# A routed expert kernel on one core: six single tiles computed in three steps of two tiles, with the routing's steps placed anew

## The chip, the core and the metric

One NeuronCore of a Trainium2 chip. Its engines run side by side and wait for each other by semaphores: TensorE (PE; matmuls, with their weight loads shown as PEld), VectorE (DVE), ScalarE (ACT), GpSimd (POOL) and SyncE (SP). The metric is the device time of one execution in microseconds (us). The kernel before takes 427.55 us, the median of 3 runs (427.18 to 428.36).

## The reference

The input x has 64 sequences of 64 tokens with 256 features, so 4096 tokens. A gate of eight experts is read from a normalised x and from a second input, each token takes the two experts of the highest gate, and their three-layer networks' outputs, weighted by the gate, are added to x:

```python
xn = rms_w * (x * jax.lax.rsqrt(var + EPS))
gate = xn @ wg_W + wg_b + (genre_embed @ gg_W + gg_b)
gate_w = jax.nn.softmax(gate, axis=-1)
topk_w, topk_i = jax.lax.top_k(gate_w, TOP_K)
cw = jnp.sum(jax.nn.one_hot(topk_i, E, dtype=x.dtype) * topk_w[..., None], axis=-2)
h1 = jax.nn.relu(jnp.einsum('bsh,ehm->bsem', x, W1) + b1)
h2 = jax.nn.relu(jnp.einsum('bsem,emn->bsen', h1, W2) + b2)
out_e = jnp.einsum('bsen,enh->bseh', h2, W3) + b3
return jnp.einsum('bseh,bse->bsh', out_e, cw)
```

W1 is 256 x 512 for each expert, W2 512 x 512 and W3 512 x 256, all in float32.

## The kernel before

Only the two chosen experts of a token are computed. Tokens of one expert are gathered into tiles of 128 rows. The kernel has a head and a tail.

The **head** first routes part A, 8 of the 32 groups of 128 tokens, which already gives two full tiles for each of the experts 1, 4 and 7. These are the six **single tiles** 0 to 5 (F = 6, HALF = 2 for each expert). Each goes through `layer1`, `layer2` and `layer3` in plain float32, where one matmul of the program leaves two records in the trace. `layer1` and `layer2` make the transposed hidden rows, four blocks m or n of 128 features, each in its own PSUM bank (PB0 to PB3), which a relu on ScalarE moves to `hid[0]` or `hid[1]`. `layer3` reads `hid[1]` as the stationary operand, and `give` on VectorE scales the result, which GpSimd later adds to the output by an indirect DMA. The rows of a tile come by a gather on GpSimd, two transposes on PE (`transpose_x`, L951) and a copy on ScalarE (L952).

Between the single tiles the routing of **part B**, the other 24 groups, is done. It is a generator, `rest()`, which a call of `more()` (the name `routing` at the top) moves on by a step. Its chain: choice of the experts on VectorE; the `ranks` and `totals`, small matmuls on PE (L433, L434, L439); VectorE's sums from L716 on, which give each entry a slot, in two halves `lo` and `hi`; four chunks c = 0 to 3 of one-hot operands on VectorE (L756, L757, L760), for which ScalarE widens `hi` (`wides`, L772) and token numbers (`tokw`, L679); 64 table matmuls on PE (L675), which sum these into one PSUM bank; then `idxR`, the token of each slot, by which unit F's rows are gathered. A transposed and turned copy `idxG` (PE L786, VectorE L802) serves the gathers of F+1 and later units, and eight steps on VectorE (L787 to L804) find the number `nex` of the first of 40 prepared shapes that fits the counts of tiles. It selects the arm of a switch in which the tail stands.

The **tail** computes the remaining tiles in **units** F, F+1, ... of up to four tiles, 512 columns. Its matmuls are float32r with split operands: high, low and a combination (`near`, L1139, and `cross`, L1154, for layers 1 and 2, `near3` and `cross3` for the third). For unit F, `transpose_part` transposes gathered rows on PE (L1190), ScalarE makes the high part (L1191) and VectorE the low part (L1192) and the combination; `split_w1` and `split_w2` split the weights (ScalarE L1081, VectorE L1084 and L1087). Units after F are transposed by two DMAs through device memory (`stow`, L926, and `shuffle`, L934) and one VectorE instruction (L943). `scales` takes the gathered gate weights, GpSimd gathers and adds throughout.

No scheduler decides the order: `tc.manual_schedule()` takes the instructions of each engine as they are written. Engines run them in that order, so a waiting instruction holds up what stands behind it on its engine. The head is written in `head_step(u, more)` for tiles 0 to 4 and `bridge()` for tile 5; each does `layer1(u)`, then `layer3(u - 1)`, then `layer2(u)`, with steps of the routing between. `layer3(5)` stands in unit F's `row`.

## Time and profile before

| | before |
|---|---|
| median of 3 runs | 427.55 us (427.18 to 428.36) |
| the profiled execution | 428.56 us |
| its span in the trace | 426.7 us |
| PE busy | 410.3 us (96%) |
| DVE, ACT, POOL busy | 343.2 (80%), 258.2 (61%), 314.0 us (74%) |
| mean granted clock of PE | 0.988 |
| share of PE in the chain that ended last | 92% |

The profile is one execution. The span runs from the first to the last instruction, and 1.86 us of the execution's time lie outside it. The start of an instruction is recorded; the end of a matmul is modelled. The granted clock is a share of 2.4 GHz. A row of the chain or of a timeline merges neighbours of one kind: "x8" are eight records. A bracket holds the idle time of the engine before the instruction and what ended it.

### The profile page before, as it was taken

How to read it: one execution, taken by the hardware profiler on the slowest of the kernel's cores; microseconds unless marked ns; L12 is line 12 of the kernel's file. 1: busy time of each engine (PE TensorE's matmuls, PEld its weight loads, DVE VectorE, ACT ScalarE, POOL GpSimd, SP SyncE). 2: the span in 40 equal slices, each digit the busy share in tenths (PEclk: the TensorE clock that was granted, in tenths of full speed). 3: DMA queues.
4: the chain of work that ended last, by engine and by line, in shares of the span. 5: the costliest groups of instructions: out<-in, count | busy, mean ns of one | idle time of the engine just before them, and what ended most of it. 6: DMA issues, size and time to landing. Idle time of an engine off the chain costs nothing.

```text
span 426.7 us, 7483 instructions
## 1 busy us (share of the span) xinstructions
PE 410.3 (96%) x2525; PEld 374.5 (88%) x2525; DVE 343.2 (80%) x545; ACT 258.2 (61%) x502; POOL 314.0 (74%) x243
## 2 busy tenths in 40 slices
...
GB/s 305 253 305 385 354 196 63 135 97 144 193 149 132 112 239 113 130 190 137 187 55 201 126 191 56 262 41 200 83 222 61 179 147 177 175 35 13 44 37 41
DMA packets 68241, 65.77 MB, mean 154 GB/s; under 512 B 35922, under 2 KB 57300, under 8 KB 67812
## 3 DMA queue, kind: packets, MB, share of 16 engines
...
## 4 chain that ended last, share of the span: by engine, by line
PE 92%; issue 2%; DMA 2%; POOL 1%; DVE 1%; ACT 1%; POOLq 0%; ACTq 0%
PE pb L1139 38%; PE pb L1154 19%; PE pb L1232 13%; PE pb L1252 6%; PE pb L1068 5%; PE pb L1056 3%; PE pb L1219 3%; POOL out_dram L1294 1%; PE pb L278 1%; DMA big<-in_x_dram 1%; PE pb L675 1%; DMA xg<-in_x_dram,idxA 1%; PE pb L309 1%; ACT pb L1147 1%; PE pb L951 0%
## 5 line engine op out<-in xcount | busy, mean ns | idle before, releaser
L1147 ACT ACTIVATE pb<-pb,bb 128x384 f32<-128x384 f32 (+7 forms) x136 | 79.5, 599 | 93.1 <-PE pb L1139 88.5
L883 POOL DMA_INDIRECT cg<-cwdR,idxR x61 | 93.1, 1527 | 18.6 <-issue 16.8
L1139 PE MATMUL pb<-h1h,w2h 128*128 128x384 f32 (+7 forms) x272 | 97.7, 360 | 0.0
L1139 PE MATMUL pb<-h1l,w2l 128*128 128x384 f32 (+7 forms) x272 | 97.4, 359 | 0.0
L1294 POOL DMA_INDIRECT out_dram<-ysE,idxR x31 | 58.3, 1881 | 11.8 <-issue 4.9
L1294 POOL DMA_INDIRECT out_dram<-ysO,idxR x27 | 49.1, 1818 | 16.1 <-ACT ysO L1275 8.1
L1179 DVE SCALAR_TENSOR_TENSOR h2l<-pb,h2h 128x384 fp32r<-128x384 f32 (+7 forms) x64 | 39.2, 617 | 26.8 <-ACT h2h L1166 19.5
L1154 PE MATMUL pb<-h1d,w2d 128*128 128x384 f32 (+7 forms) x272 | 56.4, 359 | 0.0
L1232 PE MATMUL pb<-w3h,h2h 128*128 128x256 f32 (+6 forms) x232 | 56.0, 282 | 0.0
L1232 PE MATMUL pb<-w3l,h2l 128*128 128x256 f32 (+6 forms) x232 | 56.0, 282 | 0.0
L1139 PEld LDWEIGHTS pb<-h1h,w2h 128*128 128x128 f32 x272 | 51.1, 188 | 4.4
L1139 PEld LDWEIGHTS pb<-h1l,w2l 128*128 128x128 f32 x272 | 51.2, 188 | 4.3
L1154 PEld LDWEIGHTS pb<-h1d,w2d 128*128 128x128 f32 x272 | 49.0, 188 | 4.8
L1139 PE MATMUL pb<-xh,w1h 128*128 128x384 f32 (+7 forms) x136 | 49.1, 362 | 0.4 <-ACT hid L1071 0.4
L1139 PE MATMUL pb<-xl,w1l 128*128 128x384 f32 (+7 forms) x136 | 48.7, 359 | 0.0
L883 POOL DMA_INDIRECT xgE<-in_x_dram,idxG x31 | 37.9, 1222 | 9.8 <-issue 8.8
L1166 ACT ACTIVATE h2h<-pb 128x384 fp32r<-128x384 f32 (+7 forms) x64 | 34.5, 540 | 16.8 <-PE pb L1154 13.3
L1232 PEld LDWEIGHTS pb<-w3l,h2l 128*128 128x128 f32 (+6 forms) x232 | 42.9, 185 | 0.4
L1232 PEld LDWEIGHTS pb<-w3h,h2h 128*128 128x128 f32 (+6 forms) x232 | 42.9, 185 | 0.3
L1179 DVE SCALAR_TENSOR_TENSOR h1l<-pb,h1h 128x384 fp32r<-128x384 f32 (+7 forms) x68 | 36.7, 601 | 2.4 <-ACT h1h L1163 2.3
L883 POOL DMA_INDIRECT xgO<-in_x_dram,idxG x27 | 30.2, 1119 | 8.2 <-issue 7.9
L1154 PE MATMUL pb<-xd,w1d 128*128 128x384 f32 (+7 forms) x136 | 31.9, 369 | 2.3 <-ACT pb L1147 2.2
...
## 6 DMA issues: line engine op xcount, KB each, us to landing
...
```

Source lines behind the costliest of these rows:

```text
L883: return nc.gpsimd.indirect_dma_start(out=dst, out_offset=None, in_=src, in_offset=bass.IndirectOffsetOnAxis(ap=index(b) if at is None els ...
L1056: nc.tensor.matmul(ph, lhsT=w1[:, c, ts(m, P)], rhs=cols[:, c, :], start=(c == 0), stop=(c == HC - 1))
L1068: nc.tensor.matmul(ph, lhsT=w2[:, m, ts(n, P)], rhs=hid[0][:, m], start=(m == 0), stop=(m == MC - 1))
L1139: nc.tensor.matmul(bank, lhsT=ws[t][:, c, ts(n, P)], rhs=xs[t][:, c, 0 : width(u)], start=c == 0 and t == 0, stop=c == k - 1 and t == 1, s ...
L1147: nc.scalar.activation(bank, bank, AF.Identity, bias=ww[u][1][:, l, n : n + 1], scale=1.0 + 1.0 / FINE)
L1154: nc.tensor.matmul(bank, lhsT=ws[2][:, c, ts(n, P)], rhs=xs[2][:, c, 0 : width(u)], start=False, stop=c == k - 1, skip_group_check=True,)
L1166: nc.scalar.activation(room["h2"][0][:, n, 0 : width(u)], bank, AF.Relu, scale=NEAR)
L1179: V.scalar_tensor_tensor(l, PB[n][:, 0 : width(u)], 0.0, plain(h), ALU.max, ALU.subtract)
L1219: nc.tensor.matmul(sums(u, k)[0 : cols.stop - cols.start], lhsT=native(u)[:, n, cols], rhs=w3[:, n, :], start=(i == 0), stop=(i == MC - 1),)
L1232: nc.tensor.matmul(sums(u, k)[0 : cols.stop - cols.start], lhsT=room["h2"][t][:, n, cols], rhs=room["w3"][t][:, n, :], start=n == 0 and t ...
L1252: nc.tensor.matmul(sums(u, k)[0 : cols.stop - cols.start], lhsT=room["h2"][2][:, n, cols], rhs=room["w3"][2][:, n, :], start=False, stop=n ...
L1294: add = nc.gpsimd.indirect_dma_start(out=orows, out_offset=bass.IndirectOffsetOnAxis(ap=index(b)[0 : y.shape[0]], axis=0), in_=y, in_offse ...
```

## The change

- `hid` holds 256 columns. `head_step`, `third_part` and `bridge` go, and one function `singles(more)` has the head's order. `layer1` and `layer2` take a pair q of tiles, 2q and 2q+1, 256 columns at a time; the first pair's layer 1 is done in two halves of 128 columns, since tile 1's rows come later. `layer3` of both tiles of a pair follow each other, except that `layer3(5)` still stands in unit F's row.
- The ranks and totals stand inside the second pair's layer 1 (before: inside tile 1's layer 2). The table's matmuls stand ahead of the third pair's layer 1 (16), after it (16), and after `layer3(3)` (32).
- The weights of part B's tokens are taken ahead of the last one-hot chunk. The shapes lie on 40 partitions, so the branch's steps are four on VectorE, before the table's last part; a small matmul L793 of the new file brings the marks to one row, and the turned index, the priority and `nex` follow after `idxR`.
- Unit F's second half of transposes uses PB0 and PB1; the splits of its W1 and W2 stand earlier. Adds are ordered by pairs, and gathers of x and gate weights are asked for in another order. Two more warm-up matmuls of 128 columns stand at the program's start.

```diff
-    hid = [wall.tile([P, MC, BT], F32, name=f"hid{k}") for k in range(2)]
+    hid = [wall.tile([P, MC, HALF * BT], F32, name=f"hid{k}") for k in range(2)]
...
-    shp = head.tile([1, NS, 2 * E + 1], F32, name="shp")
+    shp = head.tile([NS, 2 * E + 1], F32, name="shp")
...
-        for n in (TPB, TPB, TPB, TPB, TPB, TPB, 2, 1):
+        for n in (TPB, TPB, TPB, TPB, TPB, TPB, 2, 1, 1, 1):
...
-        prio, vm, okk = (buf(gx, [1, n], a) for a, n in (("prio", 1), ("vm", NS), ("okk", NS)))
-        viol = buf(gx, [1, NS, E], "viol")
+        prio, vm, okk = (buf(gx, [P, 1], a) for a in ("prio", "vm", "okk"))
+        viol = buf(gx, [P, 2 * E], "viol")
...
+            if c == NCH - 1:
+                pB.weights()
+                pB.spread(cwdR, cw8B, 0)
...
-        pB.weights()
-        nc.gpsimd.tensor_copy(cw8B[:, 0:NA, :], pA.cw8)
-        pB.spread(cwdR, cw8B, 0)
-        yield
-        table()
-        V.tensor_scalar(sa, tab, 0.0, float(NT + 1), ALU.is_le, ALU.mult)
-        V.scalar_tensor_tensor(idxR, tab, -1.0, sa, ALU.add, ALU.add)
-        gather_unit(F)
-        yield
-        turned, idxf = PB[7][:, P : P + NREST], t2("idxf", NREST)
-        V.tensor_copy(idxf, idxR)
-        nc.tensor.matmul(turned, lhsT=swap, rhs=idxf, start=True, stop=True)
         V.tensor_scalar(hf_i, mm, float(WQ - 1), None, ALU.add)
         V.tensor_reduce(rank, cmp, AX.X, ALU.add)
         V.tensor_scalar(hf_i, hf_i, WQ.bit_length() - 1, None, ALU.arith_shift_right)
@@ -791,17 +775,25 @@
         V.tensor_copy(hf, hf_i)
         V.tensor_tensor(cmp, hot, across(hf), ALU.mult)
         V.tensor_reduce(sL, cmp, AX.X, ALU.add)
-        near = sL[0:1].unsqueeze(1).to_broadcast([1, NS, E])
-        upper, lower = (shp[:, :, k * E : k * E + E] for k in (0, 1))
-        V.tensor_tensor(viol, near, upper, ALU.is_gt)
-        V.tensor_reduce(vm, viol, AX.X, ALU.max)
-        V.scalar_tensor_tensor(okk, vm, 0.0, shp[:, :, 2 * E], ALU.is_equal, ALU.mult)
-        V.tensor_tensor(viol, near, lower, ALU.is_le)
-        V.tensor_reduce(vm, viol, AX.X, ALU.max)
-        V.scalar_tensor_tensor(okk, vm, 0.0, okk, ALU.is_equal, ALU.mult)
+        some_viol, some_vm, some_okk, some_sL = viol[0:NS], vm[0:NS], okk[0:NS], sL[0:NS]
+        V.tensor_tensor(some_viol[:, 0:E], some_sL, shp[:, 0:E], ALU.is_gt)
+        V.tensor_tensor(some_viol[:, E : 2 * E], some_sL, shp[:, E : 2 * E], ALU.is_le)
+        V.tensor_reduce(some_vm, some_viol, AX.X, ALU.max)
+        V.scalar_tensor_tensor(some_okk, some_vm, 0.0, shp[:, 2 * E : 2 * E + 1], ALU.is_equal, ALU.mult)
+        yield
+        table()
+        V.tensor_scalar(sa, tab, 0.0, float(NT + 1), ALU.is_le, ALU.mult)
+        V.scalar_tensor_tensor(idxR, tab, -1.0, sa, ALU.add, ALU.add)
+        gather_unit(F)
+        turned, idxf = PB[7][:, P : P + NREST], t2("idxf", NREST)
+        marks = PB[7][0:1, 2 * P : 2 * P + NS]
+        V.tensor_copy(idxf, idxR)
+        yield
+        nc.tensor.matmul(turned, lhsT=swap, rhs=idxf, start=True, stop=True)
+        nc.tensor.matmul(marks, lhsT=some_okk, rhs=ident[0:NS, 0:NS], start=True, stop=True)
         V.tensor_copy(idxG, turned)
-        V.tensor_reduce(prio, okk, AX.X, ALU.max)
-        V.tensor_scalar(nex, prio, -1.0, float(NS), ALU.mult, ALU.add)
+        V.tensor_reduce(prio[0:1], marks, AX.X, ALU.max)
+        V.tensor_scalar(nex, prio[0:1], -1.0, float(NS), ALU.mult, ALU.add)
...
-    def layer1(u, between=None):
+    def layer1(q, k=None, between=()):
+        u = HALF * q
         w1, bb = ww[u][0:2]
-        w = BT
-        cols = xT[:, :, slots(u), :].rearrange("p c s t -> p c (s t)")
+        s0, own = slots(u).start, slice(0, HALF) if k is None else slice(k, k + 1)
+        cols = xT[:, :, s0 + own.start : s0 + own.stop, :].rearrange("p c s t -> p c (s t)")
+        at = slice(own.start * BT, own.stop * BT)
         for m in range(MC):
-            ph = PB[m][:, 0:w]
+            ph = PB[m][:, at]
             for c in range(HC):
                 nc.tensor.matmul(
                     ph, lhsT=w1[:, c, ts(m, P)], rhs=cols[:, c, :], start=(c == 0), stop=(c == HC - 1)
                 )
-            nc.scalar.activation(hid[0][:, m], ph, AF.Relu, bias=bb[:, 0, m : m + 1])
-            if between and m in between:
-                between[m]()
-
-    def layer2(u, between=None):
-        _, bb, w2 = ww[u][0:3]
+            nc.scalar.activation(hid[0][:, m, at], ph, AF.Relu, bias=bb[:, 0, m : m + 1])
+            if m == 2:
+                for step in between:
+                    step()
+
+    def layer2(q, between):
+        _, bb, w2 = ww[HALF * q][0:3]
         for n in range(MC):
-            ph = PB[n][:, 2 * BT : 3 * BT]
+            ph = PB[n][:, HALF * BT : 2 * HALF * BT]
             for m in range(MC):
                 nc.tensor.matmul(
                     ph, lhsT=w2[:, m, ts(n, P)], rhs=hid[0][:, m], start=(m == 0), stop=(m == MC - 1)
                 )
             nc.scalar.activation(hid[1][:, n], ph, AF.Relu, bias=bb[:, 1, n : n + 1])
-            if between and n in between:
-                between[n]()
+            for step in between.get(n, ()):
+                step()
...
-            bank = ((PB[4], PB[7]), (PB[6], PB[5]))[j][c]
+            bank = ((PB[4], PB[7]), (PB[0], PB[1]))[j][c]
...
-            if not F - 4 <= u < F and not follow(u):
+            if u % HALF == 0 if u < F - 4 else u >= F and not follow(u):
...
-        adds.append([])
+        if len(owed) % HALF == 0:
+            adds.append([])
...
+    def singles(more):
+
+        def turn_x(u):
+            return lambda: transpose_x(u)
+
+        for u in range(F):
+            stage_1(u)
+        gather(3)
+        layer1(0, 0)
+        some(len(left))
+        gates_2(((4, 5), (6, 7)), PB[7])
+        transpose_x(1)
+        gather(4)
+        for u in (0, 1):
+            gather_cw(u)
+        nc.scalar.copy(gTs, PB[7])
+        for i in late:
+            squares(i, "A")
+        layer1(0, 1)
+        last_upright()
+        layer2(0, {2: [turn_x(2)], 3: [turn_x(3)]})
+        token_numbers(0)
+        more()
+        gather(5)
+        for u in range(2, F):
+            gather_cw(u)
+        layer1(1, None, (more, more))
+        for u in (0, 1):
+            scaled(u, "A")
+            layer3(u)
+        more()
+        for u in (0, 1):
+            give(u)
+        layer2(1, {0: [more], 2: [turn_x(4)], 3: [turn_x(5), more]})
+        stream_1(F, mybir.EngineType.SP)
+        stream_2(F, mybir.EngineType.SP)
+        stream_3(F, mybir.EngineType.SP)
+        layer1(2)
+        table(2 * GC)
+        scaled(2, "A")
+        scaled(3, "A")
+        layer3(2)
+        layer3(3)
+        more()
+        stage_1(F)
+        split_w1(F, 0)
+        split_w1(F, 1)
+        for u in (2, 3):
+            give(u)
+
+        def others():
+            more()
+            turn_over()
+            gather_unit(F + 1)
+            pay()
+            pay()
+            for j in (0, 1):
+                stow(F + 1, j)
+            for j in (0, 1):
+                shuffle(F + 1, j)
+
+        layer2(
+            2,
+            {
+                0: [others, lambda: split_w2(F, 0)],
+                1: [lambda: split_w2(F, 1)],
+                2: [lambda: transpose_part(F, 0)],
+                3: [lambda: transpose_part(F, 1)],
+            },
+        )
+        scaled(4, "A")
+        layer3(4)
+        give(4)
```

The order of PE around the ranks, before (L1056 and L1068 are layers 1 and 2, L1219 layer 3, L951 a tile's transposes; `pb_68` to `pb_75` are PB0 to PB7, `w1r_81` the first expert's W1, `w1r_82` the second's):

```order
L1068 MATMUL pb_70<-hid_96,w2r_84 128x128 x4
L433 MATMUL pb_75<-incB,tri 128x8
L434 MATMUL pb_75<-incB,ntri 128x8
L439 MATMUL pb_75<-incB,ones 128x9
L1068 MATMUL pb_71<-hid_96,w2r_84 128x128 x4
L1056 MATMUL pb_68<-xT,w1r_82 128x128 x2
L1056 MATMUL pb_69<-xT,w1r_82 128x128 x2
L1056 MATMUL pb_70<-xT,w1r_82 128x128 x2
L1056 MATMUL pb_71<-xT,w1r_82 128x128 x2
L951 MATMUL pb_72<-ident,xg_226 128x128 x2
L1219 MATMUL pb_74<-w3r_87,hid_97 128x256 x4
```

and now (L1050 and L1063 are layers 1 and 2, L1217 layer 3):

```order
L1050 MATMUL pb_68<-xT,w1r_82 128x256 x2
L1050 MATMUL pb_69<-xT,w1r_82 128x256 x2
L1050 MATMUL pb_70<-xT,w1r_82 128x256 x2
L433 MATMUL pb_75<-incB,tri 128x8
L434 MATMUL pb_75<-incB,ntri 128x8
L439 MATMUL pb_75<-incB,ones 128x9
L1050 MATMUL pb_71<-xT,w1r_82 128x256 x2
L1217 MATMUL pb_73<-w3r_87,hid_97 128x256 x4
L1217 MATMUL pb_74<-w3r_87,hid_97 128x256 x4
L1063 MATMUL pb_68<-hid_96,w2r_85 128x256 x4
L1063 MATMUL pb_69<-hid_96,w2r_85 128x256 x4
L1063 MATMUL pb_70<-hid_96,w2r_85 128x256 x4
```

The ranks moved from the first pair's layer 2 into the second pair's layer 1, and two layer 3 stand between that layer 1 and its layer 2.

The order of PE from the last single tile's layer 2 on, before (L1190 transposes unit F's rows, `xgE`; unit F's first near matmuls follow):

```order
L1068 MATMUL pb_68<-hid_96,w2r_86 128x128 x4
L1190 MATMUL pb_72<-ident,xgE 128x128 x2
L1190 MATMUL pb_75<-ident,xgE 128x128 x2
L1068 MATMUL pb_69<-hid_96,w2r_86 128x128 x4
L1190 MATMUL pb_74<-ident,xgE 128x128 x2
L1190 MATMUL pb_73<-ident,xgE 128x128 x2
L1068 MATMUL pb_70<-hid_96,w2r_86 128x128 x4
L1068 MATMUL pb_71<-hid_96,w2r_86 128x128 x4
```

and now, from the last pair's layer 2 on (L1188 transposes unit F's rows, L792 turns the index, L793 brings the marks to one row):

```order
L1063 MATMUL pb_68<-hid_96,w2r_86 128x256 x4
L792 MATMUL pb_75<-idxf,swap 128x71
L793 MATMUL pb_75<-ident,okk 1x40
L1063 MATMUL pb_69<-hid_96,w2r_86 128x256 x4
L1063 MATMUL pb_70<-hid_96,w2r_86 128x256 x4
L1188 MATMUL pb_72<-ident,xgE 128x128 x2
L1188 MATMUL pb_75<-ident,xgE 128x128 x2
L1063 MATMUL pb_71<-hid_96,w2r_86 128x256 x4
L1188 MATMUL pb_68<-ident,xgE 128x128 x2
L1188 MATMUL pb_69<-ident,xgE 128x128 x2
L1217 MATMUL pb_73<-w3r_89,hid_97 128x256 x4
```

The transposes of F moved behind the third and fourth block of layer 2, the turned index came in after the first, and `layer3(4)` now stands behind the last transposes; unit F's first near matmuls follow it.

The order of VectorE at the end of the routing, before (`viol`, `vm` and `okk` test the shapes):

```order
L793 TENSOR_REDUCE sL<-cmp 128x8
L796 TENSOR_TENSOR viol<-sL,shp 1x320
L797 TENSOR_REDUCE vm<-viol 1x40
L798 SCALAR_TENSOR_TENSOR okk<-vm,shp 1x40
L799 TENSOR_TENSOR viol<-sL,shp 1x320
L800 TENSOR_REDUCE vm<-viol 1x40
L801 SCALAR_TENSOR_TENSOR okk<-vm,okk 1x40
L802 CAST idxG<-pb_75 128x71
L803 TENSOR_REDUCE prio<-okk 1x1
```

and now (L785 and L786 read the table):

```order
L777 TENSOR_REDUCE sL<-cmp 128x8
L779 TENSOR_TENSOR viol<-sL,shp 40x8
L780 TENSOR_TENSOR viol<-sL,shp 40x8
L781 TENSOR_REDUCE vm<-viol 40x1
L782 SCALAR_TENSOR_TENSOR okk<-vm,shp 40x1
L785 TENSOR_SCALAR sa<-pb_75 128x71
L786 SCALAR_TENSOR_TENSOR idxR<-pb_75,sa 128x71
L790 CAST idxf<-idxR 128x71
```

The tests of the shapes moved from behind `idxR` to ahead of it, on 40 partitions.

## Rows read from the trace of the kernel before

**Rows 1.** The page's first section, the line of TensorE: busy us, share of the span, instructions.

```profile
PE 410.3 (96%) x2525; PEld 374.5 (88%) x2525; DVE 343.2 (80%) x545; ACT 258.2 (61%) x502; POOL 314.0 (74%) x243
```

**Rows 2.** Busy time of each engine by stage: stretch, its length, then PE, PEld, DVE, ACT and POOL busy us (instructions), the granted clock of TensorE, the busy share of the DMA engines and GB/s. The two stretches are the middle of the head and the tail.

```profile
35.40:49.90 14.50, 10.68 (x64) 9.58 (x63) 12.23 (x40) 4.71 (x12) 7.54 (x8) 0.80 1.05 374
...
110.00:409.70 299.70, 299.47 (x1791) 278.61 (x1790) 260.72 (x311) 190.52 (x345) 241.95 (x157) 1.00 0.58 133
```

**Rows 3.** The chain that ended last, in order of time, 36 to 94 us: start, length, engine and line ("issue" is time in which the engine waited for nothing that the profile shows).

```profile
38.27 0.27 PE pb L433
...
38.88 0.99 PE pb L1068 x8
39.87 1.34 PE pb L1056 x12
41.21 3.58 issue
44.79 1.23 PE pb L1056 x4
...
46.44 3.41 PE pb L1219 x8
49.85 4.12 PE pb L1068 x32
53.97 1.79 PE pb L1056 x16
...
57.72 0.98 PE pb L675 x16
...
69.34 3.62 PE pb L1068 x32
72.96 2.15 PE pb L1056 x12
...
76.33 1.73 PE pb L1219 x8
...
83.17 2.63 PE pb L1139 x8
...
91.55 1.73 PE pb L1219 x8
93.28 0.93 PE pb L1139 x4
```

**Rows 4.** Busy time of each engine in single microseconds, columns as in rows 2.

```profile
45.00:46.00 1.00, 1.00 (x5) 1.00 (x6) 0.86 (x5) 0.87 (x3) 0.00 (x0) 0.50 1.06 430
...
51.00:52.00 1.00, 1.00 (x11) 1.00 (x10) 1.00 (x2) 0.37 (x1) 0.61 (x1) 1.00 0.89 363
```

**Rows 5.** ScalarE's instructions in order of time, from the stretch 35 to 92 us: start, length, line, tiles, and in brackets the idle time before it with what ended it. L1071 is the relu that reads a bank of layer 2, L952 the copy of a tile's transposed rows.

```profile
44.37 0.37 ACT L1071 ACTIVATE hid<-pb,vT 128x128 f32<-128x128 f32 x1 [4.44 <-remote]
...
54.07 0.37 ACT L1071 ACTIVATE hid<-pb,vT 128x128 f32<-128x128 f32 x1 [0.53 <-PE pb L1068]
...
58.45 0.39 ACT L952 COPY xT<-pb 128x256 f32<-128x256 f32 x1
...
70.32 0.37 ACT L1071 ACTIVATE hid<-pb,vT 128x128 f32<-128x128 f32 x1 [1.03 <-PE pb L1068]
...
75.20 0.37 ACT L1071 ACTIVATE hid<-pb,vT 128x128 f32<-128x128 f32 x1 [1.81 <-PE pb L1056]
```

**Rows 6.** VectorE's instructions in order of time, from the stretch 40 to 92 us, columns as in rows 5. L716 is the first that reads the ranks of part B; L756, L757 and L760 make one chunk of the one-hot operands; L780 reads the finished table; L1084 is one of the splits of a weight in parts of 512 columns; L1192 makes the low part of unit F's rows.

```profile
40.74 0.16 DVE L716 TENSOR_TENSOR mm<-more,pb 128x8 f32<-128x8 f32 x1 [1.69 <-PE pb L1056]
...
46.52 1.22 DVE L756 TENSOR_TENSOR big<-iotx,lo 128x2048 f16<-128x2048 f16 x1
...
49.03 0.75 DVE L760 TENSOR_TENSOR big<-big,tokw 128x1136 f16<-128x1136 f16 x1
...
55.49 0.76 DVE L757 TENSOR_TENSOR big<-tile,wide 128x1136 f16<-128x1136 f16 x1 [3.25 <-ACT wide L772]
...
67.18 0.23 DVE L780 TENSOR_SCALAR sa<-pb 128x71 f32<-128x71 f32 x1 [3.19 <-PE pb L675]
...
72.51 0.69 DVE L1084 SCALAR_TENSOR_TENSOR w1l<-w1h,w1r 128x512 fp32r<-128x512 f32 x1
...
81.81 1.56 DVE L1192 TENSOR_TENSOR xl<-pb,xh 128x256 fp32r<-128x256 f32 x4 [0.99 <-issue]
```

**Rows 7.** GpSimd's instructions in order of time, from the stretch 62 to 125 us, columns as in rows 5. The first gathers rows of unit F's first tile, the second those of the last tile of F+1, the third of F+2.

```profile
67.96 1.07 POOL L883 DMA_INDIRECT xgE<-in_x_dram,idxR  x1 [2.02 <-DVE idxf L785]
...
77.87 1.00 POOL L883 DMA_INDIRECT xgO<-in_x_dram,idxG  x1 [0.30 <-issue]
...
81.47 1.03 POOL L883 DMA_INDIRECT xgE<-in_x_dram,idxG  x1 [0.68 <-PE pb L1190]
```

**Rows 8.** The DMA queue of SyncE in order of time, from the stretch 60 to 130 us: L926 stores gathered rows of a unit (here in two halves for F+1), L934 reads them back shuffled (here for F+3).

```profile
78.13 3.60 SPq L926 DMA_DIRECT2D scr<-xgO  x2
...
115.56 0.37 SPq L934 DMA_DIRECT2D gTs<-scr  x1
```

**Rows 9.** VectorE in order of time, from the stretch 91 to 132 us: the transposition of unit F+3's shuffled rows.

```profile
126.70 1.24 DVE L943 STREAM_TRANSPOSE xT<-gTs 128x1024 f32<-128x1024 f32 x1
```

**Rows 10.** What GpSimd waited for from 95 us to the end: line, releaser, us in total, times, longest.

```profile
POOL out_dram L1294 <- ACT ysO L1275: 8.1, 1, 8.1
...
POOL out_dram L1294 <- ACT ysE L1275: 2.7, 1, 2.7
```

98 lines of the change are left out of this document (17 added, 81 removed).

## The prediction

> **What bounds the kernel now.** I read the page's busy shares first: TensorE (PE) is busy for 410.3 of 426.7 us [rows 1]. The table by stages says where the rest lies: the tail is full (299.47 of 299.70 us), while the stretch 35.4 to 49.9 us of the head lacks nearly 4 us and runs at a mean granted clock of 0.80 [rows 2]. So each microsecond that the head gives back, or loses, should move the end by as much, if nothing else in the tail is late. The chain of waits shows what the head loses [rows 3]; the reader is to compare there rows of one line with equal counts. Three losses stand out.
>
> (a) PE stands still for 3.58 us from 41.21. Behind it is a relu (L1071) on ScalarE that starts at 44.37 after 4.44 us of idling [rows 5], although the matmuls that it reads have their record's end at 39.87 [rows 3]. Layer 1 of the next tile has three of its four banks done and needs this relu's bank for the fourth.
>
> (b) After that stop the granted clock is 0.50, the 1.2 GHz level, and back at 1.00, the 2.4 GHz level, at 51 us [rows 4]. It makes layer 1's last four records 1.23 us instead of 1.79 / 4 = 0.45, layer 3's eight 3.41 instead of 1.73, and the following layer 2 4.12 instead of 3.62 [rows 3]: 0.78 + 1.68 + 0.50 = 2.96 us.
>
> (c) At the passage to unit F, layer 1 of tile 5 takes 76.33 − 72.96 = 3.37 us for work of 1.79 (loss 1.58). From 76.33 + 1.73 = 78.06 to 83.17 stand one layer 2 (3.62) and eight records of transposes (estimated at layer 2's 3.62 / 32 = 0.113 each: 0.90), so 5.11 − 4.52 = 0.59 is lost. Near and cross of unit F's first stage are 24 matmuls, at 0.93 / 4 = 0.233 each 5.58 us; they take 91.55 − 83.17 = 8.38, loss 2.80 [rows 3]. In sum 4.97 us.
>
> The losses of (c) look like that of (a): the four relus of tile 4 should follow their matmuls, but the first starts 0.08 us after the record's end (69.34 + 0.90 = 70.24 against 70.32) and the fourth 2.24 us after it (72.96 against 75.20), while a like relu at 54.07 is 0.10 late (53.97) [rows 3, 5]. I don't know why. What the rows have in common: it happens where 128-column matmuls end every 0.11 us and GpSimd issues gathers [rows 7]; it doesn't happen between 51 and 62 us, nor in the tail, where wider matmuls end every 0.23 us beside the same gathers.
>
> **The change, part by part.** The sum is made in the profiled execution, 428.56 us with a span of 426.7; it stands 1.01 us above the median of 427.55, and I carry the difference over to the median.
>
> Wider tiles. A layer 2 of two tiles is now 32 records of 256 columns at 1.73 / 8 = 0.216 [rows 3]: 6.92 instead of 2 × 3.62 = 7.24 us, 0.32 saved, three times 0.96. Layer 1 is 3.46 instead of 3.58, for two pairs (the first stays in halves): 0.24. Together **1.20 us**, all on the path.
>
> The stop, (a) and (b). In the new order the ranks stand inside layer 1 of the second pair, its fourth bank was last read by a relu a whole stage before, and two layer 3 follow, 3.46 us, which need no new relu of that stage. So nothing on PE waits there for a result made a moment before: **3.58 and 2.96 us** go. What is late next is the first layer 2 of that pair, which needs layer 1's relus, and they have those 3.46 us.
>
> The passage, (c). Layer 2 of the last pair, 256 wide, has unit F's transposes among it, and layer 3(4) stands between the last of them and the first near matmul. The 4.97 us go at best wholly; at worst they stay. VectorE decides. By the working below PE has the table's last part done at 64.6; one bank of layer 2 and the turned index's matmul later it is 66.5, and after that 3.46 of layer 2, four transposes (0.45), 1.73, four more and one layer 3 (1.73) bring PE to 74.4. VectorE makes F's index (65.4), four splits of W1 at 0.69, two output scalings at about 0.5, the turned index (69.4), four splits of W2 (72.2, if they are as long as W1's), and the low parts at 1.56 / 4 = 0.39 each [rows 6], of which the first near matmuls need three: about 73.4, or 74.0 if ScalarE's high parts of the last transposes (72.6) come first. I take 1.5 us of loss as what stays, nearer to nothing, since the wider matmuls are like those of the tail: **3.47 us** gained.
>
> What it adds. Tile 1's transposes now come right before its own half of layer 1, so PE waits for ScalarE's copy, 0.39 [rows 5] and some 0.1 around it; the same before layer 1 of the second pair, where a relu of 256 columns (about 0.5) and the copy stand between: 0.5 + 0.65 = 1.15. The 40-partition marks cost one small matmul, 0.1. Together **1.25 us** lost. If the relus are late there as in (a), up to 3.6 more; below nothing it can't be, since the covered order had no such wait. The two warm-up matmuls at the start stand before a wait for x: nothing, or at most two records, 0.2.
>
> The order of routing. In the trace layer 2 of tile 1 ends at 39.87. In the new order layer 1 of the second pair begins at about 39.87 − 1.73 (a layer 3 is later) − 0.61 (the ranks, 38.27 to 38.88) − 0.44 (columns) + 1.15 = 38.2 [rows 3]. Three quarters of it, 2.6, and the ranks, 0.6: they end near 41.4, 2.5 later than before. VectorE read them at 40.74, 1.86 after their end [rows 3, 6]; in the new order at 41.5 to 43.3. From there it needs 46.52 − 40.74 = 5.78 to the chunks, 49.78 − 46.52 = 3.26 for the first, three at 1.22 + 0.76 + 0.75 = 2.73, less what they overlap, about 2.6 each, 55.49 − 3.25 − 1.22 − 49.78 = 1.24 for expert numbers and one output scaling [rows 6], and an estimated 2 for the second scaling and the weights: 20.1, so the fourth chunk stands at 61.6 to 63.4. The 3.25 us in which VectorE waited for ScalarE's wide copies [rows 6] go, since the copies are now made one chunk ahead. PE comes to the table's last part at 38.2 + 3.46 + 0.6 + 3.46 + 6.92 + 0.5 (transposes) + 0.98 + 3.46 + 0.98 + 3.46 = 62.0 [rows 3] (0.98 for sixteen table matmuls, twice that for the last 32). So PE waits for nothing to 1.5 us; I take **0.6**. The branch counts are four small steps on 40 partitions in place of six on one; before, they stood between idxR and the turned index, now in the cover of the table's matmuls: nothing on the path, as the branch number is needed at the tail only.
>
> GpSimd. The gathers of F start after the table, 62.6 + 1.96, and 67.96 − 67.18 = 0.78 for its index [rows 6, 7]: 65.4, 2.6 before 67.96; the 0.68 us that it waited for PE at 81.47 [rows 7] go too. So GpSimd gains 3.3 where PE gains more, and falls behind PE by about 6. It has room: unit F+3's rows were asked back at 115.56 [rows 8] and transposed at 126.70 [rows 9], 11 us later; at the end it idled for ScalarE by 2.7 and 8.1 us [rows 10]. Rows of F itself land somewhere between 1.0 us (a gather's own length) and 3.9 us after a gather's start (77.87, the last of F+1, to 78.13 + 3.60, the end of the second store, which waits for it) [rows 7, 8]: with starts 1.0 + 0.3 apart the last begins at 69.3 and lands at 70.3 to 73.2, against its transposes at 72.2. Nothing, or 1.0; nothing taken.
>
> Sum: 1.20 + 3.58 + 2.96 + 3.47 − 1.25 − 0.6 = 9.36 us; 419.2 in the profiled execution, **418.2** as a median. By places, F's second stage starts at 74.4 + 5.58 + 1.73 + 1.5 = 83.2 instead of 93.28, 10.1 earlier; the 0.7 between the two are small losses before that I don't price, and the range takes them in.
>
> **A rule weighed.** The rows show relus that fall behind by 0.08 to 2.24 us over 32 records [rows 3, 5]. The Trainium skill, "TensorE: Matmul & The Clock Gate", section "The cost: per-tile semaphore tail", says that completions which each raise a semaphore are served one by one, at some 26 ns each. By it 0.11 us between records would leave no queue, so halving their number would cure nothing; the rows' growing delay isn't explained by it, and what would follow is the third rival below.
>
> **The rivals.**
> 1. All waits of (c) vanish as well, and VectorE is in time: 9.36 + 1.5 + 0.6 = 11.46, 416.1. For it speaks the full tail [rows 2]; against it that ScalarE and VectorE serve the passage in as tight an order. 0.18.
> 2. PE itself was late at (a), that is, the matmuls truly ended near 44, as the ends in the rows are modelled. The stop and the low clock come back at the ranks or at the second pair's layer 2: 6.54 lost, 424.7. Against it: VectorE's read of the ranks at 40.74, 1.86 late, lies before and not after [rows 6]. 0.10. The Trainium skill's "Perfetto Trace Analysis", section "Tensor Engine Instruction (MATMUL, LD_WEIGHTS)", says that a matmul's reported end is an estimate; no row here gives the true one.
> 3. Delayed reports don't depend on width; (c) stays whole: 418.2 + 3.5 = 421.7. 0.08.
> 4. VectorE's chain is late by 1 to 3 us more at the table's last part, as the ranks come later: about 420.5. 0.14.
> 5. GpSimd, behind by 6, holds a unit's rows or the adds at the end, which had only 2.7 us in one place [rows 10]: 3 us, 421. 0.08.
> 6. Slower. The ranks' result reaches VectorE so late that PE stands at the table's last part and the clock falls. By (a) and (b) a stop of 3.58 cost 6.54, 1.83 for each; the gain of 9.4 and another 1.3 are eaten from a stop of 5.8 us on, that is, a report 6 to 7 us late: 429 and more. The latest seen is 4.44 [rows 5]. 0.04.
>
> **How the numbers follow.** The forecast has 0.38. Faster means by over 0.3% (about 1.3 us, which is what can be told from no change), below 426.3; of the cases only the sixth, and mixtures of the second with others, end above it: faster 0.93, same 0.03, slower 0.04. The range reaches from the first rival less 0.5 (415.6) to the third and fifth with the bounds of the added waits, 423.4; it leaves out the second and sixth.
>
> **What would show it.** Right: no stop over 1 us in the chain between 35 and 62 us, the granted clock at 1.00 there, layer 2 in rows of about 0.216 us a record, near of unit F begun at 74.5 to 76 and its second stage at 82 to 84 instead of 93.28, an unchanged tail of 299 to 300 us. Wrong: a stretch of clock 0.50 at the ranks, VectorE's third and fourth chunk ended after 63, PE waiting for unit F's rows or index, or GpSimd as the releaser of waits in the tail.

## The result, and the profile after

| kernel | median of 20 runs | profiled execution | its span | mean granted clock |
|---|---|---|---|---|
| before | 428.21 us | 428.56 us | 426.7 us | 0.988 |
| changed | 425.26 us | 423.61 us | 421.8 us | 0.993 |

The ratio is 0.9917, 95% interval 0.9892 to 0.9942: the change gains 3.0 us in the medians, 4.95 in the profiled executions. 9.4 were predicted, and 425.26 lies outside the range. The ratio leaves out the executions that lie over 1.5% above the fastest of their kernel, four of them of the changed kernel (429.73 to 441.38 us), while the medians hold all 20.

The head's time went as forecast. The chain of waits of the changed kernel covers the stretch of [rows 3]; these are some of its pieces from 40 to 123 us (start, length, what):

```profile
40.80 0.23 PE pb L439 x2
...
41.99 3.45 PE pb L1217 x16
45.45 5.18 PE pb L1063 x24
...
74.30 3.76 PE pb L1134 x16
...
78.80 2.47 PE pb L1149 x8
...
82.99 7.29 PE pb L1134 x32
...
110.27 1.79 PE pb L1149 x8
112.06 0.49 issue
...
113.55 0.63 PE pb L1134 x2
...
115.34 1.62 issue
...
117.58 0.83 PE pb L1134 x4
...
118.42 2.71 PE pb L1149 x8
```

The stop of 3.58 us at 41.21 is gone, and layer 2 takes 5.18 / 24 = 0.216 us a record. Unit F's first near begins at 74.30 and its second stage at 82.99 instead of 93.28, 10.29 earlier. From there to the end of the span it is 338.81 us instead of 333.42: the tail has grown by 5.39. In the first stage of unit F+2 (L1134 at 113.55, L1149 at 118.42) there are new stops, and the eight records of 2.71 us are longer than the eight of 1.79 before them, though narrower (312 columns, not 384). The windows of one microsecond there (busy time of PE, PEld, DVE, ACT and POOL with instruction counts, then the granted clock, DMA share, GB/s):

```profile
115.00:116.00 1.00, 0.60 (x4) 0.59 (x4) 0.34 (x1) 0.00 (x0) 0.90 (x1) 1.00 0.42 127
116.00:117.00 1.00, 0.24 (x2) 0.00 (x0) 0.04 (x1) 0.49 (x1) 0.73 (x1) 1.00 0.02 8
117.00:118.00 1.00, 0.42 (x3) 0.43 (x4) 0.90 (x2) 0.12 (x1) 0.96 (x1) 1.00 0.75 61
118.00:119.00 1.00, 0.98 (x5) 0.57 (x4) 1.00 (x1) 0.72 (x2) 0.70 (x2) 0.77 1.20 234
119.00:120.00 1.00, 1.00 (x4) 0.80 (x4) 1.00 (x3) 1.00 (x4) 1.00 (x1) 0.50 0.96 238
```

PE is busy for 0.60, 0.24 and 0.42 us of three microseconds, and then the granted clock is 0.50. It is the picture of (a) and (b) of the prediction, at another place. What PE waited for shows on ScalarE; first the last cross matmuls of unit F+1's layer 2 in PE's timeline, then the relus in ScalarE's (in brackets the idle time before and what ended it):

```profile
112.55 0.97 PE L1149 MATMUL pb<-h1d,w2d 128*128 128x384 f32 x4 [0.49 <-issue]
```

```profile
114.26 0.49 ACT L1161 ACTIVATE h2h<-pb 128x384 fp32r<-128x384 f32 x1 [0.96 <-PE pb L1134]
116.44 0.49 ACT L1161 ACTIVATE h2h<-pb 128x384 fp32r<-128x384 f32 x1 [1.69 <-PE pb L1134]
```

These four end by their record at 113.52; the relu (L1161) of that bank starts at 116.44, 2.9 us later. VectorE's low part follows it at 116.96, and the near matmul that waits for it at 117.58. The near matmuls that start at 113.55 stand behind those four on TensorE, so by the recorded starts the four were done by then, and what came late is ScalarE's view of them. Such a result is called late from here on. Meanwhile GpSimd issued gathers with 0.30 us between them; two of the four gathers of x rows for unit F+4 in GpSimd's timeline:

```profile
109.84 1.04 POOL L875 DMA_INDIRECT xgE<-in_x_dram,idxG  x1 [0.30 <-issue]
111.18 1.01 POOL L875 DMA_INDIRECT xgE<-in_x_dram,idxG  x1 [0.31 <-issue]
```

### The profile page after: what moved, and what is told of

Its sections match the earlier page's. It is cut to its first block, busy times and chain, and to the rows that moved or that the text cites. A ratio compares the mean times of both kernels' runs of the same rounds, so it can differ in the third digit from the quotient of the medians.

```text
span 421.8 us, 7192 instructions
## 1 busy us (share of the span) xinstructions
PE 408.1 (97%) x2401; PEld 368.2 (87%) x2401; DVE 341.3 (81%) x543; ACT 252.5 (60%) x482; POOL 304.8 (72%) x243
## 4 chain that ended last, share of the span: by engine, by line
PE 89%; issue 3%; DVE 2%; ACT 2%; POOL 1%; DMA 1%; POOLq 0%; ACTq 0%
PE pb L1134 36%; PE pb L1149 18%; PE pb L1230 13%; PE pb L1250 7%; PE pb L1063 5%; PE pb L1050 3%; PE pb L1217 2%; POOL out_dram L1293 1%; PE pb L667 1%; PE pb L523 1%; PE pb L278 1%; DMA xg<-in_x_dram,idxA 1%; DVE xd L1114 1%; DVE xl L1110 1%; DVE h2l L1177 0%
## 5 line engine op out<-in xcount | busy, mean ns | idle before, releaser
L1134 PE MATMUL pb<-h1h,w2h 128*128 128x384 f32 (+7 forms) x272 | 97.7, 360 | 0.0
L1134 PE MATMUL pb<-h1l,w2l 128*128 128x384 f32 (+7 forms) x272 | 97.4, 359 | 0.0
L875 POOL DMA_INDIRECT cg<-cwdR,idxR x61 | 82.7, 1356 | 18.6 <-issue 17.1
L1293 POOL DMA_INDIRECT out_dram<-ysE,idxR x31 | 56.8, 1833 | 18.0 <-ACT ysE L1273 8.8
L1293 POOL DMA_INDIRECT out_dram<-ysO,idxR x27 | 47.1, 1744 | 18.4 <-ACT ysO L1273 10.8
L1177 DVE SCALAR_TENSOR_TENSOR h2l<-pb,h2h 128x384 fp32r<-128x384 f32 (+7 forms) x64 | 38.3, 615 | 26.3 <-ACT h2h L1161 20.2
L1149 PE MATMUL pb<-h1d,w2d 128*128 128x384 f32 (+7 forms) x272 | 57.4, 361 | 0.7 <-issue 0.5
L1230 PE MATMUL pb<-w3h,h2h 128*128 128x256 f32 (+6 forms) x232 | 56.4, 284 | 0.0
L1230 PE MATMUL pb<-w3l,h2l 128*128 128x256 f32 (+6 forms) x232 | 56.4, 283 | 0.0
L1134 PEld LDWEIGHTS pb<-h1h,w2h 128*128 128x128 f32 x272 | 51.1, 188 | 4.3
L1134 PEld LDWEIGHTS pb<-h1l,w2l 128*128 128x128 f32 x272 | 51.2, 188 | 4.3
L1149 PEld LDWEIGHTS pb<-h1d,w2d 128*128 128x128 f32 x272 | 48.8, 188 | 6.7 <-issue 1.1
L1134 PE MATMUL pb<-xh,w1h 128*128 128x384 f32 (+7 forms) x136 | 49.7, 366 | 2.2 <-DVE h2l L1177 1.7
L1134 PE MATMUL pb<-xl,w1l 128*128 128x384 f32 (+7 forms) x136 | 48.7, 359 | 0.0
L1161 ACT ACTIVATE h2h<-pb 128x384 fp32r<-128x384 f32 (+7 forms) x64 | 34.0, 541 | 17.1 <-PE pb L1149 12.8
L1230 PEld LDWEIGHTS pb<-w3h,h2h 128*128 128x128 f32 (+6 forms) x232 | 43.4, 187 | 0.3
L1230 PEld LDWEIGHTS pb<-w3l,h2l 128*128 128x128 f32 (+6 forms) x232 | 43.3, 187 | 0.4
L875 POOL DMA_INDIRECT xgE<-in_x_dram,idxG x31 | 36.3, 1171 | 9.4 <-issue 8.5
L875 POOL DMA_INDIRECT xgO<-in_x_dram,idxG x27 | 35.1, 1299 | 8.2 <-issue 7.0
L1119 DVE SCALAR_TENSOR_TENSOR h1d<-h1l,h1h 128x1536 fp32r<-128x1536 f32 (+7 forms) x17 | 33.6, 1974 | 0.0
```

The lines of the kernel that those rows point to most:

```text
L875: return nc.gpsimd.indirect_dma_start(out=dst, out_offset=None, in_=src, in_offset=bass.IndirectOffsetOnAxis(ap=index(b) if at is None els ...
L1119: V.scalar_tensor_tensor(d, plain(l), 1.0 / FINE, plain(h), ALU.mult, ALU.subtract)
L1134: nc.tensor.matmul(bank, lhsT=ws[t][:, c, ts(n, P)], rhs=xs[t][:, c, 0 : width(u)], start=c == 0 and t == 0, stop=c == k - 1 and t == 1, s ...
L1149: nc.tensor.matmul(bank, lhsT=ws[2][:, c, ts(n, P)], rhs=xs[2][:, c, 0 : width(u)], start=False, stop=c == k - 1, skip_group_check=True,)
L1161: nc.scalar.activation(room["h2"][0][:, n, 0 : width(u)], bank, AF.Relu, scale=NEAR)
L1177: V.scalar_tensor_tensor(l, PB[n][:, 0 : width(u)], 0.0, plain(h), ALU.max, ALU.subtract)
```

## The experiments

The runs came in sessions; kernels of one session shared a chip and the runs of the kernel before. The record gives sessions 2 and 5 the same chip number.

| session | kernel before, median (runs) | changed kernel, median (runs) | ratio, 95% interval |
|---|---|---|---|
| 1, the result | 428.21 (20) | 425.26 (20) | 0.9917 (0.9892 to 0.9942) |
| 2 | 428.32 (15) | 420.08 (1) | |
| 3 | 412.79 (25) | | |
| 4 | 425.45 (15) | 420.21 (10) | 0.9909 (0.9861 to 0.9956) |
| 5 | 412.50 (10) | 414.80 (6) | 1.0051 (1.0034 to 1.0068) |
| 6 | 429.75 (1) | | |

### Session 2: is it the tail's choice of an arm, or chance?

The first theory was that the switch to the tail's arm, prefetched earlier now, did it. Its rival was a matter of where work falls.

`e1_after_again`, the changed kernel with no edit:

> The changed kernel once more, to see whether its lost time in the tail stands at the same place. In its first trace unit F's second stage starts at 83.0 us, 10.3 earlier than before, but between 105 and 122 us 6.0 us are lost: TensorE's results are seen 2 to 3.7 us after the modelled ends of their matmuls, TensorE stops at 115 and 117 us and its granted clock falls to 0.50 for 118 to 122 us. If the loss belongs to the kernel, it stands again at unit F+2's first stage within 1 us of the same time and size (5 to 7 us). If late results fall at random, it stands elsewhere or is missing, and the span differs from 421.8 us by up to 6.

It took 420.08 us, with no stretch at the half clock: the mean clock is 0.995, and PE is busy for all of the 15 us from 110 to 125. PE's waits by what it waited for (us in total, times, longest), the largest line:

```profile
PE pb L1149 <- ACT pb L1142: 3.1, 5, 1.0
```

So one kernel's loss at this place differs from execution to execution. Of the five waits one of 0.8 stands at 77 us, at the passage to F; the others are at 110, 258, 298 and 337 us.

`e2_after_static` and `e3_before_static` (the arm isn't chosen at run time; the arm taken is always the first):

```diff
-        _, (arm,) = nc.values_load_multi_w_load_instructions(
-            nex[0:1, 0:1],
...
-        tc.switch_hint({e: arm for e in ENGS if e != ACT}, len(ARMS), "tail")
-        hints.append(lambda: tc.switch_hint({ACT: arm}, len(ARMS), "tail"))
...
-    for k in tc.Switch(arm, len(ARMS), hint="tail"):
+    for k in (0,):
```

> The changed kernel without its choice of the tail's arm: no load of the branch number, no prefetch, no switch; the one arm that these inputs take stands in the program as it is. Theory A, late results come from the switch (engines load the branch number, TensorE and the others fetch the arm): the stretches of late results at 72 to 78 and 98 to 118 us vanish, 6 to 9 us are gained against the changed kernel, so 415 to 418. Theory B, they come from what GpSimd and the DMA queues do at those times: no change beyond 1 us, 423 to 425.

> The kernel before without its choice of the arm, in the same way. Theory A: the late results at 70 to 90 us and at 106 to 115 us vanish, 3 to 5 us of the passage to unit F are gained, while the stop at 41 us stays, since it lies ahead of any branch: 422 to 425. Theory B: no change beyond 1 us.

They took 427.32 us (ratio to the kernel before 0.9975, 0.9941 to 1.0009) and 431.25 (1.0092, 1.0048 to 1.0136). Without a switch the stops are there, from the passage to F on. PE's waits in the first of them:

```profile
PE pb L1134 <- DVE h1l L1177: 5.7, 1, 5.7
PE pb L1217 <- issue: 2.5, 1, 2.5
```

The theory of the switch falls. Theory B's numbers did not come either: 427.32 is above its 423 to 425, and the kernel before without its switch is 2.9 us slower than with it. Why is open.

`e4_after_shift` (thirteen unused matmuls of 256 columns put PE 5.6 us back before the tail):

```diff
+        for k in range(13):
+            nc.tensor.matmul(
+                PB[6][:, 0:H], lhsT=hid[1][:, 0, ts(0, P)], rhs=ww[F - 1][3][:, 0, :], start=True, stop=True
+            )
         steps(F, CUT, F + len(plan))
```

> The changed kernel with 13 more matmuls of 256 columns (5.6 us) on TensorE behind layer 3 of tile 4, ahead of unit F, which write a bank that nobody reads. If the loss at unit F+2 is tied to a moment (what GpSimd, DMA queues or instruction loads do about 98 to 118 us), TensorE now comes there 5.6 us later, the loss shrinks by about as much, and the time moves by less than 2 us. If it is tied to the place in TensorE's own work, the loss stays and the time grows by 5.6 us, to 429 to 431.

Its four executions took 432.35, 435.93, 436.00 and 425.87 us, a median of 434.14. They lie further apart than the two cases of the expectation, so the time decides nothing. In the profile, of the execution of 432.35, the loss stands in unit F+1, as the window of that stretch shows:

```profile
98.00:112.00 14.00, 8.37 (x24) 5.96 (x24) 6.43 (x8) 3.91 (x8) 11.54 (x9) 0.63 0.63 180
```

From 98 to 112 us PE is busy for 8.37 of 14 us at a mean clock of 0.63. In the unshifted profile the stretch 85 to 110 is full. In these two profiles, then, the loss hits different units at some time from 98 to 121 us; `e1_after_again` shows none there, and in `e2_after_static` it stands from 62 to 98 us. At all these times GpSimd issues indirect gathers of x rows and of gate rows, with hardly a pause. That suggested theory G: results of TensorE are late while GpSimd issues indirect gathers.

### Sessions 3 and 4: GpSimd's gathers

`m1_lag`, then `f4_lag`: a kernel of its own, whose core is

```python
def run(n):
    for _ in range(n):
        k = steps[0] % 2
        bank = PB[k][:, 0:H]
        for c in range(16):
            nc.tensor.matmul(bank, lhsT=w, rhs=hs[k], start=c == 0, stop=c == 16 - 1)
        nc.scalar.copy(hs[k], bank)
        steps[0] += 1
...
mark(nc.gpsimd.tensor_copy)
for j in range(24):
    fetch(small[j % 8], scr[:, :])
run(24)
```

> A kernel of its own, with nothing of the reference computed (only its first 128 rows are written, with meaningless values): TensorE runs steps of sixteen 256-column matmuls (1.71 us at full clock), two chains in turn, ScalarE copies each step's bank out, and the step after next of the same chain needs that copy; so a result that is seen over about 1 us late stops TensorE. Beside it, in separate stretches of 24 steps with 10 quiet steps between: 24 indirect gathers of 128 rows of 32 bytes by GpSimd; 24 indirect gathers of 128 rows of 1 KB by GpSimd; 24 plain DMAs of 128 rows of 32 bytes issued by GpSimd; three plain loads of 1 MB on SP's queue; and the 1 KB gathers together with six such loads. Theory G (TensorE's results are seen 2 to 4 us late while GpSimd issues indirect DMAs): in the stretches one, two and five TensorE waits for ScalarE by 1 to 3 us a step in a good part of the steps (busy share under 0.85), in three and four it is at 1.00 as in the quiet ones. Rival T (the traffic of the DMA queues does it): stretches four and five show the waits, one does not. Rival W (it belongs to the kernel's own matmul widths and handovers, not to GpSimd): no stretch shows a wait over 0.3 us.

> The kernel of its own again (steps of sixteen 256-column matmuls in two chains, ScalarE copying out, GpSimd idle or issuing gathers of 32 bytes a row, gathers of 1 KB a row, plain DMAs; then plain loads on SP's queue, then gathers with loads; nothing of the reference is computed). Where the kernel before takes 412 to 414: TensorE busy 0.99 or more in every stretch, 424.8 us of span, as in the call before. Where it takes 426 to 430, theory G: waits for ScalarE of 1 to 3 us in the stretches with gathers, none in the quiet ones, and a span of 435 or more; rival W (only the kernel's own narrow and mixed handovers show it): 425 again.

A step took 1.92 us, not the 1.71 of the expectation. In session 3 there were no waits and the span was 424.8 us. In session 4 the same kernel had 491.2. Windows of both, columns as above; of the first, the stretch of gathers of 32 bytes a row:

```profile
52.30:83.40 31.10, 31.10 (x261) 31.10 (x261) 0.00 (x0) 5.97 (x16) 24.09 (x24) 1.00 0.06 4
```

and of the second, gathers of 32 bytes a row, gathers of 1 KB, plain DMAs from GpSimd, a piece of the plain loads on SP's queue, gathers of 1 KB once more, and a quiet stretch:

```profile
52.60:83.80 31.20, 17.70 (x117) 16.91 (x115) 0.00 (x0) 2.23 (x6) 24.10 (x24) 0.70 0.07 4
140.90:171.90 31.00, 14.36 (x105) 13.66 (x104) 0.00 (x0) 2.23 (x6) 23.94 (x24) 0.76 0.34 98
226.00:239.00 13.00, 13.00 (x111) 13.00 (x110) 0.00 (x0) 2.36 (x7) 12.76 (x25) 1.00 0.13 9
...
302.00:316.00 14.00, 14.00 (x119) 14.00 (x119) 0.00 (x0) 2.62 (x8) 0.00 (x0) 1.00 0.89 336
357.50:388.60 31.10, 16.51 (x112) 15.81 (x111) 0.00 (x0) 2.23 (x6) 24.02 (x24) 0.74 0.34 98
400.00:480.00 80.00, 80.00 (x669) 80.00 (x668) 0.00 (x0) 15.30 (x42) 0.00 (x0) 1.00 0.01 1
```

PE loses 13.5, 16.6 and 14.6 us beside the gathers and nothing anywhere else, not at 336 GB/s of plain loads either. Packets and traffic are out as a cause by themselves. Gathers beside heavy loads were not measured: the loads of the fifth stretch were issued from 302.02 to 316.06, and its gathers began at 357.49, so it repeats the second. ScalarE's timeline in the first of these stretches shows how the wait grows while the gathers run, which end at 83.74:

```profile
57.07 0.37 ACT L88 CAST h<-pb 128x256 fp32r<-128x256 f32 x1 [1.55 <-PE pb L87]
59.85 0.37 ACT L88 CAST h<-pb 128x256 fp32r<-128x256 f32 x1 [2.41 <-PE pb L87]
65.56 0.37 ACT L88 CAST h<-pb 128x256 fp32r<-128x256 f32 x1 [5.34 <-remote]
76.84 0.37 ACT L88 CAST h<-pb 128x256 fp32r<-128x256 f32 x1 [10.91 <-remote]
```

1.55 us is the idle time of an undisturbed step; then the idle times are 2.41, 5.34 and 10.91. TensorE's timeline tells whether the matmuls or their reports were late:

```profile
59.82 2.92 PE L87 MATMUL pb<-h,w 128*128 128x256 f32 x23
65.99 3.79 PE L87 MATMUL pb<-h,w 128*128 128x256 f32 x16 [3.25 <-ACT h L88]
```

The copies come one for each step of sixteen matmuls, in order. The one at 65.56 releases the step that starts at 65.99; the next one, at 76.84, reads the step that ends by its record at 62.74. TensorE takes its matmuls in order, and the whole step from 65.99 was started in between. So the matmuls were done, and their report came about 14 us late.

`e5_no_gates` in session 3, then `f3_no_gates` in session 4 (the gates of tiles F and later are zeros, but for the first row of each):

```diff
     V.memset(cgR, 0.0)
...
-            fetch(cg, (cwdA if b < F else cwdR)[:, :], b)
+            if b < F:
+                fetch(cg, cwdA[:, :], b)
+            else:
+                nc.gpsimd.dma_start(cg[0:1], cwdR[0:1, :])
```

> The changed kernel, with the indirect gathers of gate rows of tiles F and later replaced by a plain DMA of one row of 32 bytes from GpSimd (the gates of these tiles are zeros, so their experts' part is missing from the output); matmuls, evictions, adds and the gathers of x rows stay. Theory G: there is no indirect gather between about 84 and 97 us any more, late reports stay only beside the gathers of x rows and the adds, and the loss of 5.96 us at unit F+2's first stage falls to 0 to 3: 418 to 421 us. Rival T (DMA traffic): the gate rows are under 4 KB each, so nothing changes: 424 to 426. Rival V (it varies by chance from execution to execution, not by what GpSimd does): 422 to 426 with a spread as before, 420 to 430.

> The changed kernel, with the indirect gathers of gate rows of tiles F and later replaced by a plain DMA of one row of 32 bytes from GpSimd (the gates of these tiles are zeros, so their experts' part is missing from the output). On a chip where the kernel before takes 412 to 414: 413.6 to 414.7 again, nothing to tell. Where it takes 426 to 430, theory G (late results beside indirect gathers): 418 to 421, the stop at F+2 under 3 us; rival (late results whatever GpSimd does): 423 to 426.

In session 3, without late results, it took 414.16 us where the kernel before takes 412.79, 1.0027 of it; the changed kernel has 1.0051 in session 5. So where nothing is late, leaving these gathers out is worth about 1 us at most. In session 4 it took 415.80 (0.9776 of the kernel before, 0.9719 to 0.9833), and

`f2_after_again`, the changed kernel beside it, with no edit,

> The changed kernel, beside the kernel before on one chip. Theory L: what the change gains is the late results' cost, so on a chip without them it gains nothing: 412.5 to 414.5 beside 412.8 (the three kernels made from it took 413.96 to 414.81 there); on a chip with them 3 us, 425 beside 428. Rival (the change takes out the VectorE work and the order that made the stops, whatever the chip): 4 to 9 us on either, 404 to 409 beside 412.8.

took 420.21, 5.2 us less than the kernel before, where 3 had been expected. So fewer indirect gathers give back 4.4 us, and 415.80 lies a little below the 418 to 421 that I had expected; the slowest of its four executions (416.53) is faster than the fastest of the ten with the gathers (417.39). In the changed kernel's profile of session 4 F+2's first stage, in the chain, still has gaps:

```profile
115.00 0.22 issue
...
115.78 0.90 issue
```

and PE is busy for 13.86 of the 15 us from 110 to 125; without the gate gathers it is full there:

```profile
110.00:125.00 15.00, 15.00 (x111) 15.00 (x109) 13.04 (x19) 10.16 (x21) 12.09 (x12) 1.00 0.77 180
```

`f1_before_again`, the kernel before with no edit:

> The kernel before, for a second profile of it: its 15 runs of the first call here had a median of 428.32 us and its 25 runs of the second call 412.79, so the time that both kernels take depends on the chip by 15 us, five times what the change is worth. Theory L: on one chip TensorE's results are seen 2 to 4 us late in stretches, on the other not. If these runs are of the kind of 412 to 414, this profile has no stop at 42 to 46 us and none at the passage to F, no stretch at the half clock, and its second stage of F starts at 83 to 85 us, not 93.28; if of the kind of 426 to 430, the stops of the first profile come again within 3 us of their places.

Its span is 425.8. The stop of the head is back in the chain, and GpSimd's timeline has gathers ahead of it, such as:

```profile
41.58 2.60 issue
```

```profile
39.08 1.00 POOL L883 DMA_INDIRECT cg<-cwdA,idxA  x1 [0.31 <-issue]
```

`e6_gates_plain` in session 3, then `g2_gates_plain` in session 5 (plain DMAs of 128 fixed rows in place of the gate gathers):

```diff
+                i = (b - F) % 24 * P
+                nc.gpsimd.dma_start(cg, cwdR[i : i + P, :])
```

> The changed kernel, with the same indirect gathers of gate rows (tiles F and later) replaced by plain DMAs from GpSimd of 128 fixed rows of 32 bytes each (so the gates of these tiles are those of other tokens): as many instructions and packets, without the indirect addressing. Theory G: as without them, 418 to 421 us, late reports only beside the gathers of x rows and the adds. Rival P (any DMA that GpSimd issues does it, by its descriptors or its packets): as the changed kernel, 424 to 426. If this one is slow and the one with a single row is quick, it is the packets and not the indirect form.

> The changed kernel, with the indirect gathers of gate rows (tiles F and later) replaced by plain DMAs from GpSimd of 128 fixed rows of 32 bytes each (so the gates of these tiles are those of other tokens). Theory G, on a chip where the kernel before takes 425 or more: 414 to 417, 3 to 5 us under the changed kernel, as with the single rows (415.8 beside 420.2): it is the indirect form, not the DMA's packets. Rival P (any DMA issued by GpSimd): as the changed kernel. Where the kernel before takes 413: 414 again.

413.96 and 414.02 us, both in sessions without late results: inconclusive for G.

`e8_no_fills` in session 3:

```diff
-        f = nc.sync.dma_start(our[:, i : i + NB // NF, :], xr[:, i : i + NB // NF, :])
+        f = nc.sync.dma_start(our[:, i : i + 1, 0:8], xr[:, i : i + 1, 0:8])
```

> The changed kernel, with the four copies of x into the output of 768 KB each on SP's queue (after the first eight columns) cut to 32 bytes a row, so that the output lacks x in most rows. Rival T (the DMA queues' traffic delays the reports): the reports are in time, the weights come earlier, and the loss at F+2 goes: 417 to 420 us. Theory G: the late reports beside GpSimd's gathers at 67 to 86 and 97 to 118 us stay, and the time stays at 423 to 426; a gain of up to 1 may come from the first stages, where rows and weights wait for the queue.

414.81 us; inconclusive for the same reason.

### Sessions 5 and 6: what the change is worth by itself, and what the gathers need to do harm

`g4_after_beside`, the changed kernel with no edit:

> The changed kernel once more, beside the others on their chip. Where the kernel before takes 425 to 429: 418 to 426, 0.985 to 0.996 of it. Where it takes 412 to 414 (theory L: what the change gained was the cost of late results): 412.5 to 415, 0.999 to 1.005 of it, with no stop over 1 us behind ScalarE or VectorE after 40 us; the rival there (the shorter chains gain by themselves): 404 to 409.

414.80 us, 2.3 more than the kernel before beside it, as theory L has it: in the one session without late results that has both, the change makes the kernel slower. Its profile (span 413.5) against that of session 1 (second row), the windows from 110 to 125 us:

```profile
110.00:125.00 15.00, 15.00 (x112) 14.97 (x110) 14.55 (x20) 11.16 (x23) 12.86 (x8) 1.00 0.74 164
```

```profile
110.00:125.00 15.00, 12.50 (x67) 10.49 (x67) 8.60 (x15) 7.40 (x16) 12.26 (x10) 0.89 0.82 181
```

112 matmuls were begun in the same time instead of 67. F's second stage begins at 81.45 in the one and at 82.99 in the other; the spans differ by 8.3 us.

`g3_later` (the rows of F+4 are gathered behind the adds of F; nothing is left out):

```diff
-        if u <= F + 1:
+        if u <= F + 2:
             gather_unit(u + 2)
             stow(u + 2)
...
-        further = u > F and u + 3 < last
+        further = u > F + 1 and u + 3 < last
```

> The changed kernel with one pair exchanged in the tail, nothing left out: the gathers of x rows of unit F+4 stand behind the adds of unit F on GpSimd, so none is issued while F+2's first stage runs (108 to 115 us in the profiles). Theory G, on a chip where the kernel before takes 425 or more: F+2's first stage meets fewer late results and the loss there falls by 1 to 3 us: 417 to 419 beside 420 of the changed kernel. Rival (the late results come with the adds as well, or the shuffle of F+4 gets late): no gain, 420 to 422.

423.24 us (1.0267, 1.0249 to 1.0284), 8.4 more than the changed kernel beside it: a miss, and by a cause of its own. PE waits once for 7.1 us; the chain there, from the last gather through the two passes of the rows' turning is this; layer 3 (L1250) stands behind the turned rows on VectorE and begins at 141.65:

```profile
128.44 2.85 DMA xgE<-in_x_dram,idxG
...
131.36 4.04 DMA scr<-xgE
...
135.46 4.27 DMA gTs<-scr
```

The rows came too late; the session had no late results to save.

`g1_lag2` in session 5, then `h2_lag2` in session 6, the second kernel of its own; of its stretches, those with something between the gathers are

```python
for j in range(16):
    fetch(small[j % 8], scr[:, :])
    nc.gpsimd.tensor_copy(rest[1], rest[0])
...
for j in range(24):
    fetch(small[j % 8][0:32], scr[:, :], 32)
```

> A kernel of its own (nothing of the reference is computed): steps of sixteen 256-column matmuls in two chains, each step's bank copied out by ScalarE for the step after next. Beside 24 steps each, GpSimd issues: 24 gathers of 128 rows of 32 bytes back to back; 16 such gathers with a GpSimd copy of 128x256 behind each; 12 with three such copies behind each; 24 gathers of 32 rows; 18 indirect adds of 128 rows of 1 KB; and 24 gathers of 128 rows while VectorE copies out instead of ScalarE. On a chip where the earlier kernel of this kind took 491 us: theory G with a backlog (the reports queue behind the gathers and catch up in the pauses): the waits of TensorE are 12 to 15 us in the first stretch, under 6 with one copy, under 2 with three, under 5 with 32 rows, 2 to 8 beside the adds, 12 to 15 with VectorE as with ScalarE. Rival (each gather costs a fixed delay, without a backlog): the waits go with the number of gathers, so 16 gathers with copies cost two thirds and 12 a half of the first stretch. Rival (the delay is ScalarE's own): none in the stretch with VectorE. On a chip where it took 425 us: no wait anywhere.

> The second kernel of its own again (steps of sixteen 256-column matmuls in two chains; gathers back to back, with one copy between, with three, of 32 rows, adds, and gathers with VectorE copying out; nothing of the reference is computed); it took 478.8 us in a call where the kernel before takes 412.5. Where the kernel before takes 425 or more, theory G with a backlog: waits of TensorE of 12 to 15 us in the first stretch, under 6 with one copy between, under 2 with three, under 5 with 32 rows, 2 to 8 beside the adds, 12 to 15 with VectorE copying out. Rival (a fixed delay for each gather): two thirds of the first stretch with one copy, a half with three. Rival (ScalarE alone sees them late): none with VectorE. Where the kernel before takes 412 to 414: 478.8 again, no wait.

In session 5 PE was full in every stretch (span 477.0). In session 6 (552.5) the windows are, in the order of the expectation (the third, with three copies, is full as well and left out):

```profile
34.00:65.50 31.50, 17.96 (x117) 16.96 (x115) 0.00 (x0) 2.24 (x6) 24.34 (x24) 0.73 0.07 4
125.60:150.90 25.30, 25.30 (x213) 25.30 (x213) 0.00 (x0) 4.85 (x13) 22.66 (x32) 1.00 0.05 4
...
263.90:292.80 28.90, 10.03 (x70) 9.62 (x68) 0.00 (x0) 1.12 (x3) 21.80 (x24) 0.73 0.03 2
362.00:434.40 72.40, 72.40 (x606) 72.40 (x605) 0.42 (x1) 13.43 (x36) 28.16 (x19) 1.00 0.28 32
434.70:465.90 31.20, 14.51 (x104) 13.81 (x102) 2.46 (x6) 0.00 (x0) 24.14 (x24) 0.76 0.11 8
```

Back to back PE loses 13.5 us. With one GpSimd copy behind each gather it loses nothing. That is within the expectation (under 6), and a fixed price for each gather, two thirds of 13.5, falls. Gathers of 32 rows are no better (18.9 lost, where under 5 was expected). VectorE in ScalarE's place loses 16.7, so the delay isn't ScalarE's. The adds lose nothing, where 2 to 8 was expected, but here each waits for the one before it, 4.2 us from start to start; in the kernel they stand 1.9 apart, so they aren't cleared. GpSimd's timeline in the second stretch shows how little lies between:

```profile
125.62 1.03 POOL L99 DMA_INDIRECT small<-scr,idx  x1 [0.53 <-issue]
126.66 0.41 POOL L118 COPY rest<-rest 128x256 f32<-128x256 f32 x1
127.23 1.03 POOL L99 DMA_INDIRECT small<-scr,idx  x1 [0.17 <-issue]
```

A gather every 1.61 us, with a copy between, does no harm; one every 1.3 (31.5 / 24) stops PE. Whether the copy or the longer distance does it wasn't told apart.

`h1_before_third`, the kernel before with no edit:

> The kernel before, for a profile of it in a call where it takes 412 to 414. Theory L (without late results the change only costs: wider tiles and the gaps at a set of loads): no stop at 42 to 46 us and none behind ScalarE or VectorE at 70 to 82; its second stage of F starts 1.5 to 3 us before the changed kernel's 81.45 of such a call, at 78.5 to 80; F+2's first stage and all after it lead by the same amount, with no further difference over 0.5 us; span 410 to 411.5. Rival (the tail differs too): second stage at 81 to 82 and a lead that grows behind 110. Where this call is one of 425 to 429: second stage at 90 to 94 again.

It fell into a session with late results: 436.28 us, again with the stop in the head (3.04 us at 39.59); at the passage the chain has a piece of 4.12 at 84.15, a wait of ScalarE, and F's second stage starts at 99.43, later than the 90 to 94 expected. So there is no profile of the kernel before from a session without them.

## Why the prediction was wrong

**Right in time: the head.** The wider tiles came to 0.216 us a record; (a) and (b) went; the 0.6 us set aside for VectorE's chain weren't needed; the added waits for ScalarE's copies are 1.1 us in two pieces, with 1.25 taken; F's index, rows and GpSimd's lead gave no wait. Of (c) I let 1.5 us stay: against the profile without late results (81.45) F's second stage is 1.54 late. It began 10.29 us earlier than in the profile before, 83.2 forecast and 82.99 measured. That the 1.5 fits is luck: `e1_after_again` has it too, the profiles of `f2_after_again` and `e4_after_shift` have nothing of it, and in `e2_after_static` F's second stage starts at 91.25.

The reason given for (a) and (b) is only half of it. I expected VectorE to read the ranks at 41.5 to 43.3, up to 1.9 us late as before, and nothing to wait for them. The ranks end at 41.03, and they are read at once:

```profile
41.07 0.16 DVE L708 TENSOR_TENSOR mm<-more,pb 128x8 f32<-128x8 f32 x1 [2.84 <-PE pb L1050]
```

So results weren't late there at all, though GpSimd issues five gathers from 35.55 to 41.76 with 0.30 us between. The profiles of `e1_after_again`, `e2_after_static`, `e4_after_shift` and `f2_after_again` show the same. Before, an add and one more gather followed, up to 44.66; now GpSimd does nothing then. No run tells whether the new order on PE or that on GpSimd ended the stop.

**The step that failed: the unchanged tail.** The condition "if nothing else in the tail is late" was taken for granted, with an unchanged tail of 299 to 300 us, and under it stood the inference that late results belong to 128-column matmuls which end every 0.11 us. I had seen GpSimd's gathers in the rows and set them aside, because the tail's wider matmuls ran full "beside the same gathers". In the tail of the kernel before it went well, but for 0.8 us of waits in F+1, at the places where the gathers fell. The change moves PE 10 to 11.5 us forward and GpSimd by 4.3 at F+4's gathers (109.84 instead of 114.16 us in the trace before), so that these gathers meet F+2's first stage, 312 columns wide, where each bank's relu and low part are needed at once. That this meeting is the cause is argued from the places; `g3_later`, which was to test it, ran in a session without late results. From layer 3 of F (L1232 at 109.59 before, L1230 at 98.09 now) to that of F+1 (127.10 and 121.13), with F+2's first stage between them, the lead falls from 11.5 to 6.0 us, and at the end it is 4.9. Of the rivals, the third came nearest (the delay doesn't depend on width), with another place; the fifth (GpSimd behind by about 6 us) named the shift but not its effect. The second, that PE itself is late, is out by the recorded starts: in the kernel of its own a whole step was started before the copy of the step ahead of it. The rows before the change had it already [rows 3, 5]: twelve records of the next layer 1 start from 39.87 on, and the relu of the matmuls ahead of them at 44.37.

By the medians, if all of the difference between sessions 1 and 5 is put down to late results, which isn't shown: they cost the kernel before 428.21 − 412.50 = 15.7 us and the changed kernel 425.26 − 414.80 = 10.5. The change then saves 5.2 of them, where (a), (b) and (c) in the prediction made 10.0, and costs 2.3 by itself, where the rest of my sum (1.20 − 1.25 − 0.6) made a cost of 0.65. That 5.2 − 2.3 gives the measured 3.0, within rounding, follows from how the two are formed and checks nothing. In session 4 the same account has 13.0 and 5.4, so the size of the saving varies.

**What is shown and what is open.** Shown, in kernels of their own and in two sessions of four: indirect gathers back to back delay the reports of PE's matmuls to ScalarE or VectorE, whatever their bytes, and nothing else that was tried does. Shown in the kernel: without the gate gathers it is 4.4 us faster in such a session, and about 1 us at most in one without late results. That the remaining gathers, of x rows and of the head, cause the rest of the loss is argued by where they stand. Open is why some sessions have it and others don't, under one chip number too; why the tail is full in long stretches beside such gathers (85 to 109 us in the changed kernel's profile); which 2.3 us the change costs (the copies' waits are 1.1 of them at most); and whether a GpSimd instruction between the kernel's gathers would free it, which wasn't tried. No version that was run beats both kernels in both kinds of session.
